# A two-layer graph network: the last batch's preparation, the order of its norm, values and products, and where single-value transfers are issued

## The chip, the cores and the metric

The kernel runs on one core of one Trainium2 chip. The metric is the device time of one execution in microseconds (us). A core has five engines that run their own instruction queues in order and meet by semaphores: PE (matmul), DVE (vector), ACT (scalar activations), POOL (GpSimd) and SP, which here only issues DMA transfers. POOL and ACT issue transfers too.

## What is computed

Eight batches of 2048 tokens with 256 features, and one 2048 by 2048 adjacency matrix for all. Two layers, each with a norm ahead of it and a residual:

```python
# layer 0: attention in 4 heads, a softmax for each chunk of 256 keys
h = maximum(layernorm(x), 0)
q, k, v = h @ Wq.T + bq, h @ Wk.T + bk, h @ Wv.T + bv      # split into heads
s = clip(q @ k.T / sqrt(64), -10, 10); s = where(adj == 0, -10, s)
ctx = sum over chunks of softmax(s within the chunk) @ v
out = ctx @ Wo.T + bo + h
x = x + layernorm(out) * gamma + beta
# layer 1: one graph-attention step
h = maximum(layernorm(x), 0) @ W
e = leaky_relu(h @ a1 [row] + h @ a2 [column], 0.01); e = where(adj == 0, -1e9, e)
x = x + relu(softmax(e) @ h)
```

A row of `adj` without any neighbour gives equal weights, so such a token gets the mean of all `h` instead.

## The kernel before, in words

Tokens come in four blocks of 512 (`NNB` = 4), called zero, low, mid and last; a block is four tiles of 128 tokens. The instruction order on each engine is written by hand: what the program emits first on an engine runs first there. Tiles of one tag share a few buffers, and an instruction that takes a buffer waits for the last user of it.

**Setup.** The first batch is projected to q, k and v; in between, `find` turns rows of `adj` into flags (DVE, with a copy on POOL), `bound` turns them over on PE and has ACT write them as int8 bounds (`keep_bounds`, line 314). Parts that don't stay on the chip are put on a list, and `send_bounds` (line 304) issues them to DRAM from POOL. It is called at the end of each `find` and once more at the end of the setup. The pieces `att.early(0..3)` start the attention meanwhile; `early(2)` holds the first sum on POOL.

**Attention frames.** Attention runs in steps, one for each pair of block and key chunk, 32 a batch. `begin(f)` and `end(f)` form frame f, f = 2 to 34: logits of one step (line 503), clip on DVE (543), exponentials on ACT (552), sums of pairs on POOL (`both`, 558), value products on PE (519), sums on PE (531), reciprocals on ACT (563, 564), scaling on DVE (573), and `gather` (578), a transfer from POOL that accumulates into `ctxT`. All other work is put beside it by half-frame: `at(n, piece)` has the piece run in frame n // 2, in its second part where n is odd. `PER` is 16 half-frames for a block and `STEPS2` is 64.

A block's work between the layers is in the class `Between`: `load` fetches x; `residual` makes the layer's input again by the first norm (ACT, line 379); `bias` and `beta` add two constant rows to it and to x (lines 748, 772); `output` multiplies the context by Wo; `take` (741) adds residual and output; `stats`, `power`, `shift`, `scaled`, `gamma` (768) and `add` (776) are layer 0's last norm; `stats1`, `power1`, `shift1`, `norm1` are layer 1's first. In the frames `bias`, `beta`, `gamma` and `add` run on POOL, after them on DVE. `beside()` gives the half-frames for blocks zero, low and mid, counted from the end of the block's own steps. Block last has its load, residuals, bias and beta in the frames around n = 58 to 69.

**Between the layers.** After the frames comes a list for each engine order, one for batches with a next one (`ahead`) and one for the last batch. `flip1`, `send1` and `fetch1` turn a normed block by way of DRAM; `ends(0)` turns it on PE instead (`turn1`, `keep1`, line 799), `ends(1)` makes the four tiles of h (`values`, line 827) and keeps them (`keep`: ACT 835, DVE 836). Layer 1's scores need e by row and by column: `targets` works on columns (ACT 916, 917); rows go through DRAM as single values (`send`, line 921, 512 values of four bytes) and come back to all partitions (`receive`, line 925, then `received`, line 934), or by PE (`sources`).

**Layer 1.** `weights(i)` (DVE, lines 953 and 959) makes the i-th of 16 tiles of weights: four pairs of instructions in two halves. `products(i)` (PE, line 976) multiplies it: 32 matmul records; i = 4 nb + j4 for query block nb and quarter j4 of the keys. In the last quarter PE goes by token groups, and a group needs both halves of the weights. In the last batch `early(i)` does products 0 to 2 before the loop. `mean` (PE 903, ACT 907) makes the average row, `alone(nb)` (DVE) adds it to tokens without neighbours, `finish` (994 to 999) scales and adds on POOL. In the last batch the loop starts at i = 3.

Of the kernel before, what the change touches and what calls it, by code (L numbers as in the profile page):

```python
# [28 lines left out]
def gnn_two_layers(  # L29
# [656 lines left out]
    class Between:  # L686
# [160 lines left out]
                    self.values(t)  # L847
                    self.keep(t)

        def beside(self):  # L850

            todo = {
                -3: [self.load],
                3: [lambda: self.residual(0)],
                4: [lambda: self.residual(1)],
                5: [lambda: self.bias(0)],
                6: [lambda: self.bias(1)],
                8: [pe(lambda: self.output_tiled(0)), lambda: self.stats([0]), lambda: self.beta(0)],
                9: [
                    pe1(lambda: self.output_tiled(1)), after_clips(lambda: self.take(0)),  # L860
                    after_clips(lambda: self.take(1)), lambda: self.stats([1]),
                ],
                10: [lambda: self.stats([2]), lambda: self.beta(1)],
                11: [lambda: self.stats([3])],
                12: [self.power],
                13: [self.shift],
                14: [lambda: self.scaled(range(TB))],
                15: [lambda: self.gamma(0)],
                16: [lambda: self.gamma(1)],
                18: [lambda: self.add(0)],  # L870
                20: [lambda: self.add(1)],
            }

            def at(n, *pieces):
                todo.setdefault(n, []).extend(pieces)

            if self.nb == NNB - 2:
                return todo
            at(22, lambda: self.stats1([0]))

            at(25, first(lambda: self.stats1([1, 2, 3])))
            at(26, self.power1)
            at(27, self.shift1)
            at(28, lambda: self.norm1(0))
            at(29, lambda: self.norm1(1))
            at(30, lambda: self.flip1(0))
            at(31, lambda: self.flip1(1))
            at(33, self.send1)
            return todo
# [217 lines left out]
    find(20, 21)  # L1107
    bound(18, 19)
    proj.qk(NNB - 1, 1)
    att.early(2)  # L1110
    bound(20, 21)
    find(22, 23)
# [35 lines left out]
    for b in range(B):  # L1148
# [21 lines left out]
            of[HALVES_OF[k % 8]] = fetch_bounds(HALVES_OF[k % 8])  # L1170

        for nb in range(NNB - 1):
            for n, pieces in blocks[nb].beside().items():
                at((nb + 1) * PER + n, *pieces)
        if b == 0:
            for n, pieces in once.items():
# [14 lines left out]
                at(n + 7, lambda nb=nb: ahead.send(nb))  # L1191
        for k in range(8):
            at(8 * k + (40 - 24 if b == 0 and k == 3 else 12), lambda k=k: fetch(k + 3))
        at(STEPS2 - 6, last.load)
        at(STEPS2, lambda: last.residual(0))

        late = 0 if ahead else 2
        at(STEPS2 + 1 + late, lambda: last.residual(1))
        at(STEPS2 + 2, lambda: last.bias(0))
        at(STEPS2 + 3 + late, lambda: last.bias(1))  # L1200
        at(STEPS2 + 4, lambda: last.beta(0))
        at(STEPS2 + 5, lambda: last.beta(1))
        at(STEPS2 + 3, low.fetch1)
        if ahead:
            at(STEPS2 - 4, lambda: ahead.fetch(0))
# [29 lines left out]
        if ahead:  # L1235
            for t in range(TB):
                mid.stats1([t])
                low.values(t)
                low.keep(t)
            low.sum1()  # L1240
            zero.fetch1()
            mid.power1()
            mid.shift1()
            mid.norm1(0)
            mid.norm1(1)
            ahead.values(0)
            ahead.fetch(2)
            last.output(0)
            last.output(1)
            mid.flip1(0, "both")  # L1250
            last.take(0)
            mid.flip1(1)
            last.take(1)
            mid.send1()
            zero.sum1()
            last.stats(range(TB))
            ahead.qk(1, 0)
            last.power()
            last.shift()
            last.scaled(range(TB))  # L1260
            ahead.qk(1, 1)
            for t2 in range(2):
                last.gamma(t2)
                last.add(t2)
            for t in range(TB):
                last.stats1([t])
                zero.values(t)
                zero.keep(t)
            mid.fetch1()
            last.power1()  # L1270
            last.shift1()
            last.norm1(0)
            last.norm1(1)
            ahead.values(1)
            ahead.qk(2, 0)
            last.flip1(0, "both")
            last.flip1(1)
            last.send1()
            ahead.fetch(3)
            mid.sum1()  # L1280
            ahead.qk(2, 1)
            mid.ends(1)
            last.fetch1()
            one.send(1)
            one.send(2)
            ahead.values(2)
            one.receive(1)
            one.targets(0, 3 * TB)
            one.sources(0)
            ahead.qk(3, 0)  # L1290
            weights(0)
            ahead.qk(3, 1)
            last.sum1()
            last.ends(1)
            one.total()
            one.targets(3 * TB, NT)
            weights(1)
            one.send(3)
            ahead.values(3)
        else:  # L1300
            one.targets(0, TB)
            one.sources(0)
            weights(0)
            low.ends(1)
            low.sum1()
            mid.stats1(range(TB))
            mid.power1()
            mid.shift1()
            accs[0] = one.accumulators(0)
            early(0)  # L1310
            mid.norm1(0)
            mid.norm1(1)
            one.targets(TB, 2 * TB)
            last.output(0)
            last.output(1)
            weights(1)
            last.take(0)
            last.take(1)
            mid.ends(0)
            mid.ends(1)  # L1320
            last.stats(range(TB))
            last.power()
            last.shift()
            last.scaled(range(TB))
            one.targets(2 * TB, 3 * TB)
            one.send(1)
            one.receive(1)
            for t2 in range(2):
                last.gamma(t2)
                last.add(t2)  # L1330
            last.stats1(range(TB))
            last.power1()
            last.shift1()
            weights(2)
            fetch(11)
            last.norm1(0)
            last.norm1(1)
            early(1)
            last.ends(0)
            last.ends(1)  # L1340
            early(2)
            one.total()
            one.targets(3 * TB, NT)
            weights(3)
            one.mean()
            one.received(1)
            one.send(2)
            one.send(3)
            one.receive(2)
            weights(4)  # L1350
            fetch(12)
# [4 lines left out]
        for i, (nb, j4) in enumerate(pieces1):  # L1356
            if not ahead and i < 3:
                continue
            if i + 2 < len(pieces1):
                weights(i + 2)  # L1360
            if i % 2 == 0 and (ahead or i < 10):
                fetch(i // 2 + 11)
            if nb not in accs:
                accs[nb] = one.accumulators(nb)
            if j4 == 1 and nb + 1 < NNB:
                one.received(nb + 1)
                if nb + 2 < NNB:
                    one.receive(nb + 2)
            if j4 == 2:
                one.alone(nb)  # L1370
            one.products(accs[nb], ws.pop(i), j4)
            if ahead and i == 0:
                one.mean()
            if j4 == 0 and nb > 0:
                one.finish(nb - 1, accs[nb - 1])
            if j4 == 1 and nb > 0:
                one.store(nb - 1)
            if far and i in (3, 6, 9, 12):
                far.send(i // 3 - 1)
            if far and i in (0, 3, 6, 9):  # L1380
                far.load(i // 3)
            if far and i in (1, 4, 7, 10):
                far.stats(i // 3, range(TB))
                far.power(i // 3)
                far.shift(i // 3)
            if far and i in (2, 5, 8, 11):
                for t2 in range(2):
                    far.norm(i // 3, t2)
                for t2 in range(2):
                    far.flip(i // 3, t2)  # L1390
            if ahead and i == len(pieces1) - 4:
                att = Attention(ahead)
            if ahead and i >= len(pieces1) - 4 and i < len(pieces1) - 1:
                att.early(i - (len(pieces1) - 4))
                if i == len(pieces1) - 2:
                    att.early(3)
# [34 lines left out]
```

## Time and profile before

| what | value |
|---|---|
| median of 3 runs | 3537.56 us (3534.24, 3537.56, 3537.88) |
| the profiled execution, own time | 3534.5 us |
| its span, first to last instruction | 3532.7 us |
| PE busy | 3512.5 us, 99% |
| DVE busy | 2632.9 us, 75% |
| ACT busy | 1945.8 us, 55% |
| POOL busy | 1825.8 us, 52% |
| bytes moved | 330.29 MB, mean 93 GB/s |

The profile gives, for one execution, when each instruction ran on its engine and what released it. A line of a timeline has the start, the time, the engine, the source line, the operation, the tiles it writes and reads, and in brackets how long the engine was idle before and what ended that. "x32" means so many instructions put together. A line of the waits has who waited for whom, the total in us, the number of times and the longest. The clock is the share of full speed that PE was granted; over the span its mean was 0.999.

### The profile page before, as it was taken

How to read it: one execution, taken by the hardware profiler on the slowest of the kernel's cores; microseconds unless marked ns; L12 is line 12 of the kernel's file. 1: busy time of each engine (PE TensorE's matmuls, PEld its weight loads, DVE VectorE, ACT ScalarE, POOL GpSimd, SP SyncE). 2: the span in 40 equal slices, each digit the busy share in tenths (PEclk: the TensorE clock that was granted, in tenths of full speed). 3: DMA queues.
4: the chain of work that ended last, by engine and by line, in shares of the span. 5: the costliest groups of instructions: out<-in, count | busy, mean ns of one | idle time of the engine just before them, and what ended most of it. 6: DMA issues, size and time to landing. Idle time of an engine off the chain costs nothing.

```text
span 3532.7 us, 104631 instructions
## 1 busy us (share of the span) xinstructions
PE 3512.5 (99%) x46104; PEld 2370.3 (67%) x46104; DVE 2632.9 (75%) x3979; ACT 1945.8 (55%) x2961; POOL 1825.8 (52%) x1198
## 2 busy tenths in 40 slices
PE   9999999999999999999999999999999999999989
PEld 5455775667777687566867758656686665855768
DVE  6887677877678676786767868678586785867866
ACT  6777426763267633676236762477624766047740
POOL 5677017870278602785037850378404883058731
PEclk9999999999999999999999999999999999999999
DMA  7545323443144431444324343243432434223421
GB/s 245 126 109 123 93 84 75 97 114 98 62 92 86 115 99 61 92 92 109 97 66 88 86 121 104 61 84 81 120 99 67 86 83 114 60 61 80 102 62 45
DMA packets 178521, 330.29 MB, mean 93 GB/s; under 512 B 36752, under 2 KB 98448, under 8 KB 178064
## 3 DMA queue, kind: packets, MB, share of 16 engines
q1 hardware_dynamic: 136912, 203.51, 18.9%
q0 software_dynamic: 32832, 119.03, 18.4%
q8 instruction: 361, 5.91, 0.7%
q10 hardware_dynamic: 8320, 1.05, 0.2%
q14 instruction: 96, 0.79, 0.1%
HBM read 154.67 MB, written 51.43 MB: 58 GB/s over the span
## 4 chain that ended last, share of the span: by engine, by line
PE 98%; DVE 1%; ACT 1%; DMA 0%; issue 0%; POOL 0%; ACTq 0%; DVEq 0%; POOLq 0%
PE ps_s L503 25%; PE ps_n L519 25%; PE ps_s L976 12%; PE ps_t L531 7%; PE ps_n L976 6%; PE ps_t L976 6%; PE ps_t L727 2%; PE ps_t L447 2%; PE ps_n L447 2%; PE ps_s L447 2%; PE ps_n L827 2%; PE ps_t L827 2%; PE ps_n L461 1%; PE ps_t L461 1%; PE ps_t L705 0%; PE ps_n L705 0%
## 5 line engine op out<-in xcount | busy, mean ns | idle before, releaser
L543 DVE SCALAR_TENSOR_TENSOR e<-ps_s,bound 128x1024 f32<-128x1024 f32 x1024 | 1217.6, 1221 | 399.8 <-PE ps_s L503 395.7
L558 POOL TENSOR_TENSOR both<-e 128x1024 f32<-128x1024 f32 x512 | 1220.2, 2410 | 546.9 <-PE ps_t L531 238.1
L503 PE MATMUL ps_s<-q,k 64*32 64x512 f32 x16384 | 1328.4, 590 | 0.1
L552 ACT ACTIVATE e<-e 128x1024 f32<-128x1024 f32 x1024 | 1049.2, 1049 | 453.9 <-DVE e L543 436.3
L519 PE MATMUL ps_n<-e,v 64*32 64x512 f32 x16384 | 1114.6, 589 | 2.1 <-DVE prod L573 1.4
L503 PEld LDWEIGHTS ps_s<-q,k 64*32 64x32 f32 x16384 | 524.0, 106 | 386.5 <-issue 248.7
L519 PEld LDWEIGHTS ps_n<-e,v 64*32 64x32 f32 x16384 | 556.9, 107 | 332.0 <-issue 200.0
L531 PE MATMUL ps_t<-both,ones 64*32 64x512 f32 x4096 | 553.2, 590 | 0.0
L976 PE MATMUL ps_s<-g,w 128*128 128x257 f32 x2048 | 450.2, 381 | 5.0 <-DVE w L959 5.0
L976 PEld LDWEIGHTS ps_s<-g,w 128*128 128x128 f32 x2048 | 389.4, 190 | 61.8 <-DVE w L959 5.4
L573 DVE TENSOR_TENSOR prod<-ps_n,rz 128x512 f32<-128x512 f32 x448 | 288.9, 687 | 133.4 <-ACT rz L564 70.9
L999 POOL TENSOR_TENSOR x<-x,r 128x256 f32<-128x256 f32 x124 | 90.7, 745 | 469.3 <-ACT r L997 468.5
L959 DVE SCALAR_TENSOR_TENSOR w<-bound,w 128x1024 f32<-128x1024 int8 x256 | 314.7, 1229 | 8.7
L367 POOL TENSOR_TENSOR krn<-krn,mv 128x4 f32<-128x4 f32 x28 | 6.8, 243 | 571.7 <-DVE w L953 571.7
L976 PE MATMUL ps_n<-g,w 128*128 128x257 f32 x1024 | 292.4, 382 | 0.0
L976 PE MATMUL ps_t<-g,w 128*128 128x257 f32 x1024 | 289.8, 380 | 0.0
L563 ACT ACTIVATE rz<-ps_t 128x512 f32<-128x512 f32 x256 | 152.6, 596 | 226.2 <-PE ps_t L531 140.3
L953 DVE TENSOR_SCALAR w<-src,cd 128x512 f32<-128x512 f32 x512 | 268.7, 567 | 9.9 <-ACT src L934 7.0
L531 PEld LDWEIGHTS ps_t<-both,ones 64*32 64x32 f32 x4096 | 156.3, 105 | 100.5 <-SPq L475 43.8
L976 PEld LDWEIGHTS ps_n<-g,w 128*128 128x128 f32 x1024 | 192.8, 190 | 44.3 <-issue 17.6
L578 POOL DMA_DIRECT2D ctxT<-prod x224 | 191.0, 853 | 53.4 <-DVE prod L573 46.9
L976 PEld LDWEIGHTS ps_t<-g,w 128*128 128x128 f32 x1024 | 193.8, 189 | 28.2
(139 smaller groups left out, 2970.1 us busy)
## 6 DMA issues: line engine op xcount, KB each, us to landing
ctxT<-prod POOLq DMA_DIRECT2D x224, 512.0 KB, 4.9
bound<-bound_d SPq DMA_DIRECT2D x125, 512.0 KB, 4.8
turned_d<-squares SPq DMA_DIRECT2D x232, 128.0 KB, 2.9
hT<-turned_d SPq DMA_DIRECT2D x58, 512.0 KB, 4.5
rows<-in_adj_dram SPq DMA_DIRECT2D x32, 512.0 KB, 5.2
x<-in_x_dram SPq DMA_DIRECT2D x32, 512.0 KB, 6.4
out_dram<-x SPq DMA_DIRECT2D x31, 512.0 KB, 2.6
xp<-in_x_dram SPq DMA_DIRECT2D x28, 512.0 KB, 4.3
```

The source lines that it names most:

```text
L447: nc.tensor.matmul(in_key_order(pp) if i == 0 else pp, w[:, di, do * P:(do + 1) * P], h, start=di == 0, stop=di == FC - 1,)
L503: nc.tensor.matmul(self.s[n, o][c * Q:(c + 1) * Q, kt, :], self.k[p][rows, at:at + Q], self.q[p][rows, nb * NB:(nb + 1) * NB], start=True, ...
L519: made.append(nc.tensor.matmul(self.num[n, c][h * Q:(h + 1) * Q, :], self.v[rows, j * KT + kt, at:at + Q], self.e[n, p][rows, i * KT + kt, :],
L531: nc.tensor.matmul(self.total[n][h * Q:(h + 1) * Q, :], ones[rows, :], self.both[n, h // 2][rows, h % 2, :], start=half == 1, stop=half == 0,)
L543: nc.vector.scalar_tensor_tensor(self.e[n, p][:, i * KT:(i + 1) * KT, :], self.s.pop((n, o)), -CLIP * SC, bounds[nb, j // 4][:, j % 4 * KT ...
L552: nc.scalar.activation(e, e, AF.Exp, scale=1.0 / SC)
L558: nc.gpsimd.tensor_tensor(self.both[n, p], e[:, 0], e[:, 1], op=ALU.add)
L573: nc.vector.tensor_tensor(dst[:, c, :], self.num.pop((n, c)), self.rz[n], op=ALU.mult)
L578: nc.gpsimd.dma_start(self.ctxT[nb], self.prod.pop(n), accum_op=ALU.add)
L953: nc.vector.tensor_scalar(w[:, i, :], self.src[nb], self.cd[:, 0, j:j + 1], self.cd[:, 1, j:j + 1], op0=ALU.mult, op1=ALU.max,)
L959: nc.vector.scalar_tensor_tensor(two, bounds1[nb, j // 8][:, j % 8 - 1:j % 8 + 1, :], 0.0, two, op0=ALU.is_gt, op1=ALU.mult)
L976: nc.tensor.matmul(accs[t][:, 0:F + 1], w[:, i, t * P:(t + 1) * P], g[:, j, :], start=j == 0, stop=j == NT - 1,)
```

## The change

- In the setup, one more call of `send_bounds()` stands between the last projection of k and `att.early(2)`.
- In the last batch block mid's two `add` pieces move from half-frames 66 and 68 to 65 and 66.
- In the last batch block last's seven pieces move: load from 58 to 37, residuals from 64 and 67 to 42 and 43, bias from 66 and 69 to 49 and 51, beta from 68 and 69 to 59 and 60. In the other batches the list has the half-frames that they had.
- In batches with a next one, `send(1)` moves ahead, right behind block mid's `send1`; `send(2)` moves behind `weights(1)`.
- In the last batch's list, block mid's values and keeps are put around the `power` and `shift` of block last, `weights(2)` and a fetch of bounds stand ahead of block last's `scaled`, and products 1 and 2 come earlier: 1 ahead of `stats1`, 2 ahead of block last's `ends`. The mean moves behind products 3, in the loop.
- In the last batch `alone(0)` is added behind it. Before, the loop skipped i = 2, where this step stands.

```diff
+            soon = soon and self.nb == NNB - 2
+            at(17 if soon else 18, lambda: self.add(0))
+            at(18 if soon else 20, lambda: self.add(1))
...
     proj.qk(NNB - 1, 1)
+    send_bounds()
     att.early(2)
...
-            for n, pieces in blocks[nb].beside().items():
+            for n, pieces in blocks[nb].beside(soon=ahead is None).items():
...
-        at(STEPS2 - 6, last.load)
-        at(STEPS2, lambda: last.residual(0))
-
-        late = 0 if ahead else 2
-        at(STEPS2 + 1 + late, lambda: last.residual(1))
-        at(STEPS2 + 2, lambda: last.bias(0))
-        at(STEPS2 + 3 + late, lambda: last.bias(1))
-        at(STEPS2 + 4, lambda: last.beta(0))
-        at(STEPS2 + 5, lambda: last.beta(1))
+        early_parts = [58, 64, 65, 66, 67, 68, 69] if ahead else [37, 42, 43, 49, 51, 59, 60]
+        last_parts = [
+            last.load, lambda: last.residual(0), lambda: last.residual(1), lambda: last.bias(0),
+            lambda: last.bias(1), lambda: last.beta(0), lambda: last.beta(1),
+        ]
+        for n, piece in zip(early_parts, last_parts):
+            at(n, piece)
...
             mid.send1()
+            one.send(1)
             zero.sum1()
...
             last.fetch1()
-            one.send(1)
-            one.send(2)
             ahead.values(2)
...
             weights(1)
+            one.send(2)
             one.send(3)
...
             mid.ends(0)
-            mid.ends(1)
             last.stats(range(TB))
-            last.power()
-            last.shift()
+            for t in range(TB):
+                if t == 2:
+                    last.power()
+                    last.shift()
+                mid.values(t)
+                mid.keep(t)
+            one.targets(2 * TB, 3 * TB)
+            weights(2)
+            fetch(11)
             last.scaled(range(TB))
-            one.targets(2 * TB, 3 * TB)
             one.send(1)
             one.receive(1)
             for t2 in range(2):
                 last.gamma(t2)
                 last.add(t2)
+            early(1)
             last.stats1(range(TB))
             last.power1()
             last.shift1()
-            weights(2)
-            fetch(11)
             last.norm1(0)
             last.norm1(1)
-            early(1)
+            early(2)
             last.ends(0)
             last.ends(1)
-            early(2)
             one.total()
             one.targets(3 * TB, NT)
             weights(3)
-            one.mean()
             one.received(1)
...
             one.products(accs[nb], ws.pop(i), j4)
-            if ahead and i == 0:
+            if i == (0 if ahead else 3):
                 one.mean()
+            if not ahead and i == 3:
+                one.alone(0)
```

More of the change, by code (lines that the diff above doesn't have):

```diff
@@ L848, in ends, with beside @@
                     self.keep(t)
-        def beside(self):
+        def beside(self, soon):
             todo = {
@@ L869, in beside @@
                 16: [lambda: self.gamma(1)],
-                18: [lambda: self.add(0)],
-                20: [lambda: self.add(1)],
             }
```

## The prediction

> **What bounds the kernel now.** I read the page's slices and chain first, then the waits of PE, then PE's timeline around its gaps, and there DVE, POOL and ACT.
>
> From the page, the slices and the chain by engine:
>
> ```profile
> PE   9999999999999999999999999999999999999989
> ...
> PE 98%; DVE 1%; ACT 1%; DMA 0%; issue 0%; POOL 0%; ACTq 0%; DVEq 0%; POOLq 0%
> ```
>
> PE is the bound nearly everywhere; only slice 39 (3356 to 3444 us) falls below nine tenths. So an edit counts only where PE now idles, or where it newly makes PE idle. The waits of PE alone say where (total, times, longest):
>
> ```profile
> PE ps_s L976 <- DVE w L959: 5.0, 1, 5.0
> PE ps_n L388 <- ACT hn L379: 4.6, 1, 4.6
> ...
> PE ps_n L519 <- ACT bound_part L314: 0.8, 1, 0.8
> ```
>
> The first two lie between the two layers of the last batch. PE's timeline there:
>
> ```profile
> 3387.86 1.03 PE L827 MATMUL ps_t<-w1s,hT 128*128 128x258 f32 x4
> 3393.85 8.74 PE L976 MATMUL ps_s<-g,w 128*128 128x257 f32 x32 [4.96 <-DVE w L959]
> ...
> 3410.99 7.10 PE L976 MATMUL ps_s<-g,w 128*128 128x257 f32 x32
> 3422.71 1.95 PE L388 MATMUL ps_n<-ident,hn 128*128 128x128 f32 x4 [4.61 <-ACT hn L379]
> ...
> 3437.94 7.12 PE L976 MATMUL ps_s<-g,w 128*128 128x257 f32 x32
> ```
>
> The same 32 products take 8.74 and 7.10 us. The table by stretches, cut where the clock changes, has the reason (columns: PE, PEld, DVE, ACT, POOL busy, granted clock, DMA share, GB/s):
>
> ```profile
> 3393.58:3397.00 3.42, 3.15 (x7) 2.51 (x8) 3.35 (x11) 0.00 (x0) 0.00 (x0) 0.50 0.00 0
> ...
> 3417.47:3420.89 3.42, 0.63 (x3) 0.19 (x2) 3.18 (x11) 0.00 (x0) 0.00 (x0) 1.00 0.00 0
> 3420.89:3427.71 6.82, 4.95 (x13) 3.15 (x14) 4.57 (x8) 4.31 (x12) 0.00 (x0) 0.50 0.00 0
> ```
>
> After each gap PE runs at half clock, 3.4 and 6.8 us long. Why the first gap exists, from DVE's and POOL's timelines:
>
> ```profile
> 3386.11 6.43 DVE L953 TENSOR_SCALAR w<-src,cd 128x512 f32<-128x512 f32 x2 [0.43 <-ACT src L934]
> ...
> 3393.72 1.00 DVE L953 TENSOR_SCALAR w<-src,cd 128x512 f32<-128x512 f32 x2
> ```
>
> ```profile
> 3385.98 0.86 POOL L578 DMA_DIRECT2D ctxT<-prod  x1 [5.60 <-DVE prod L573]
> 3386.58 1.56 POOL L776 TENSOR_TENSOR x<-x,o 128x512 f32<-128x512 f32 x1
> ...
> 3390.26 1.53 POOL L772 TENSOR_TENSOR x<-x,beta_r 128x512 f32<-128x512 f32 x1
> ```
>
> The same pair takes 6.43 us beside four POOL additions and 1.00 us without them; one instruction took 5971 ns against a median of 541, until POOL ended at 3391.79. The third wait is in the setup:
>
> ```profile
> 69.00 3.54 POOL L304 DMA_DIRECT2D bound_d<-bound_part  x4
> 74.03 1.94 ACT L314 ACTIVATE bound_part<-ps_z 128x1024 int8<-128x1024 bf16 x2 [3.94 <-DMA bound_d<-bound_part]
> 76.02 2.45 PE L519 MATMUL ps_n<-e,v 64*32 64x512 f32 x26 [0.77 <-ACT bound_part L314]
> ```
>
> ACT waits there for a transfer that POOL issued late, and PE for ACT.
>
> [...] a window that was 18% busy (0.63 of 3.42) lowered the clock too, and one of 60% (2.03 us of 3373.1 to 3376.5) didn't. [...] the 2 KB send of single values lands here after a median 10.2 us.
>
> **The change part by part**, against the profiled execution (3534.5 us, span 3532.7). Times are of its clock.
>
> *Setup, one early send.* ACT finishes the two parts at 62.27 + 1.93 = 64.2, so POOL issues both by 65.2 (0.88 each). They land after at most 6.8 us (longest of this transfer in the trace), by 70.1 and 71, instead of 73.9. ACT, free at 70.1, evicts 22 and 23 by 72.1 and exponentiates by 74; PE wants that at 75.65. The cost: POOL's first sum and the two copies of z behind it come up to 2 us later, the second ending at 69.8 instead of 69.1, so its eight transposes start at 69.85 instead of 69.24: +0.6. From its first logits of frame 2 (73.31) PE issued 96 records until 81.45; at the pace of full frames (32 records in 1.72 us) they need 5.15, so 3.0 us were lost. Now 73.9 + 5.15 = 79.05, and by DVE's second clip (ends 78.2) 79.15. Gain 2.3; bounds -0.6 (only POOL's delay is felt) and 2.9.
>
> *Seven batches with a next one: sends.* One send follows the middle block's turned squares, another goes behind the weights. PE has no idle there (20.00 busy of 2964 to 2984 and of 2984 to 3004). The last block's fetch landed 7.89 us after issue beside two sends, the middle one's 3.51 without, yet at 2995.05 it was early for PE's 2997.69. The send on SP ahead of the middle fetch is issued at about 2964.6 and done near 2975; that fetch starts at 2973.36 (it waits for PE) and is wanted at 2983.44. Cost and gain 0; the early list for these batches equals the old slots.
>
> *Last batch, frames.* The last block's two norms (ACT, 1.08 each) go to half-frames 42 and 43, its four POOL additions to 49, 51, 59, 60, its load to 37. Two additions in one frame exist in the old kernel (POOL at 3253.88 and 3255.13): the sums behind them start 0.06 late. The frame of 59 has two and a shift, 0.55 late, with 0.25 to spare before PE; frame 21 delays ACT's reciprocal by 0.35, which DVE's multiplication half covers. I take +0.2, bounds 0 and 3.
>
> *Last batch, between the layers.* After 3385.98 POOL has only the gather left.
> - DVE's first instruction did not get in at 3386.11 although the first addition began at 3386.58, so I let the gather hold it to 3386.84 (bounds 0 and 0.85). The first half of the weights then ends at 3389.1 (0.54 + 0.52 + 1.22 on), and DVE's chain is 4.67 ahead of before.
> - PE: products 0 from 3389.2 (6.95) to 3396.15, output 3.46 to 3399.6, transposes to 3400.5. The middle block's values need the bank that `take` frees at 3406.90 - 4.67 = 3402.25: a gap of 1.8. Values 3.5 to 3405.8.
> - Only two values go ahead of `power`; ACT and DVE reach weights 2 at 3407.15, done at 3411.6. PE needs them at 3412.75, behind products 1. The old 4.6 us wait for the last norm is covered: DVE goes on at 3411.55, and gamma to norm takes 8.06 as before, so to 3419.6, while products 2 end at 3419.7. Transposes and values as before for the middle block (1.38 + 3.73): 3424.8.
> - What is late next: products 3, with nothing before them now. Weights 3 start 2.12 after the last value matmuls start (before: 3429.26 to 3431.38), at 3426.05; their halves end 2.25 and 4.44 later, 3428.3 and 3430.5. The first token group needs both: PE idles 3.5, runs 0.87, idles 1.3, and ends products 3 at 3430.55 + 6.08 = 3436.65. The mean, moved behind them, 0.87: products 4 at 3437.5, against 3437.94 + 6.95 = 3444.9. Gain 7.4.
> - That new gap will cost clock: a half-clock window costs up to 1.7, part of it inside the gap. I take 1.2; bounds 0.4 and 3.4 (two windows).
> - The four new `alone` steps stand on DVE between weights 5 and 6, behind the mean, done about 3440.5; weights 6 end at 3445, wanted at 3451. Free. `fetch` 11 stands ahead of send 1 and receive 1 on SP, waits for weights 1 until 3401.6; receive lands near 3415, wanted at 3426. Free.
>
> Sum: 2.3 + 7.4 - 1.2 - 0.2 = 8.3, so 3526.2 on the profiled execution's time. The median of the runs, 3537.56, is 3.1 above it; on that, 3529.
>
> **The rivals.**
> - A, the late wait costs more: two half-clock windows (3.4), and the setup gives nothing: 7.4 - 3.4 = 4.0, 3533.5. [...] against: the setup wait has one plain cause.
> - B, POOL wasn't what held DVE: the 4.67 stay, and only the reordering pays: 2.7 + 2.3 - 1.2 = 3.8, 3534. Against: one instruction of 512 took 5971 ns, and it ended with POOL.
> - C, slower: the single-value send stands ahead of the middle block's fetch in seven batches. It decides if that fetch lands over 10.1 us after issue (2983.44 - 2973.36); each us beyond costs 7. At the longest landing of such a send, 12.6, it costs 17.5, so 3546. For: the last fetch took 7.89 beside two; against: this send is nearly done when the fetch starts, so 10.1 isn't near.
> - That the sends don't do what they are moved for: the last fetch will land in about 3.5 instead of 7.9 us, and nothing waits for it. This is in the forecast.
>
> **How the numbers follow.** Forecast 0.72 (own range 3525 to 3532), A 0.14, B 0.08, C 0.06. What can be told from no change is about 0.2%, 7 us, so faster means below 3530.5. Of the forecast's cases about 0.63 lie there, 0.09 above; with A and B that gives faster 0.63, same 0.31, slower 0.06. The range 3524 to 3536 takes in A and B and leaves out C.
>
> **What would show it.** Right: the first pair of the last batch's weights takes 1 to 2 us; the 4.96 and 4.61 waits are gone; a wait of products 3 for weights of 3 to 5 us stands after the last values, then half clock; the setup's products of frame 2 don't wait for a bound part. Wrong: PE gaps in the seven earlier batches (C), a pair still at 6 us (B), or frames 21 to 30 of the last batch over 7.73 us.

## The result, and the profile after

The changed kernel takes 3527.6 us in the median of 11 runs (3524.82 to 3531.08), the kernel before 3536.22 in 11 runs on the same chip (3534.24 to 3537.88). The ratio is 0.9977, its 95% interval 0.9967 to 0.9986: 0.23% faster. The profiled execution took 3525.83 us with a span of 3524.1, 8.6 less than the span before.

The page's slices and chain after:

```profile
PE   9999999999999999999999999999999999999999
...
PE 98%; DMA 1%; DVE 0%; ACT 0%; POOL 0%; issue 0%; ACTq 0%; DVEq 0%; POOLq 0%
```

The slice that was at 8 tenths is full now. The waits of PE after (total, times, longest):

```profile
PE ps_s L977 <- DVE w L960: 3.5, 1, 3.5
PE ps_n L1035 <- POOL ident masks.py:199: 1.5, 1, 1.5
PE ps_n L519 <- DVE prod L573: 1.4, 1, 1.4
```

The waits of 5.0 and 4.6 are gone and one of 3.5 has come; the other two lines stand at the kernel's start and in the last frames, as before. Lines of the kernel behind 876 have moved down by one (953 is 954, 959 is 960, 976 is 977). PE's timeline between the layers of the last batch, after:

```profile
3386.16 1.03 PE L827 MATMUL ps_t<-w1s,hT 128*128 128x258 f32 x4
3387.03 7.10 PE L977 MATMUL ps_s<-g,w 128*128 128x257 f32 x32
...
3398.80 1.28 PE L827 MATMUL ps_n<-w1s,hT 128*128 128x258 f32 x4 [0.34 <-ACT hT L799]
...
3402.53 14.04 PE L977 MATMUL ps_s<-g,w 128*128 128x257 f32 x64
3416.41 0.84 PE L388 MATMUL ps_n<-ident,hn 128*128 128x128 f32 x4
...
3425.40 10.12 PE L977 MATMUL ps_s<-g,w 128*128 128x257 f32 x32 [3.48 <-DVE w L960]
3435.36 1.02 PE L904 MATMUL ps_n<-w1s,hsum 128*128 128x256 f32 x4
```

Products 0 follow the values at once, at full clock (7.10 us, granted clock 1.00). Products 1 and 2 run as one block of 64. Then products 3 (the line at 3425.40) wait 3.48 us and take 10.12. DVE and POOL at the start of weights 0, after:

```profile
3384.41 1.00 DVE L954 TENSOR_SCALAR w<-src,cd 128x512 f32<-128x512 f32 x2 [0.43 <-ACT src L935]
```

```profile
3384.28 0.86 POOL L578 DMA_DIRECT2D ctxT<-prod  x1 [6.82 <-DVE prod L573]
```

The pair that took 6.43 us takes 1.00, although the gather on POOL runs beside it. In the trace of before PE's clock changes between the layers at 3393.58, 3397.00, 3417.47, 3420.89 and 3427.71, which lie whole multiples of 3.41 us apart; a "window" below is one such 3.41 us. The windows around the new wait (columns as in the table of before):

```profile
3420.62:3424.04 3.42, 1.30 (x6) 0.78 (x5) 1.56 (x7) 1.77 (x5) 0.00 (x0) 1.00 0.07 1
3424.04:3427.45 3.41, 2.05 (x4) 1.17 (x4) 3.38 (x5) 0.00 (x0) 0.00 (x0) 0.50 0.23 77
3427.45:3430.87 3.42, 3.30 (x9) 2.67 (x9) 3.35 (x6) 0.00 (x0) 0.00 (x0) 0.50 1.03 80
```

PE was busy for 1.30 of 3.42 us, and two windows at half clock followed.

Where the time came from, read from both traces at four marks on PE:

| stretch | before | after | gain |
|---|---|---|---|
| start to layer 1 of batch 0 | 403.41 | 401.81 | 1.60 |
| six batches, from there to layer 1 of batch 6 | 2601.22 | 2600.67 | 0.55 |
| from there to the last values of block low (line 827) | 383.23 | 383.68 | -0.45 |
| from those values to products 4, "between the layers" | 57.04 | 50.06 | 6.98 |

The gains sum to 8.68; from products 4 to the last instruction both need 87.83 us. One part of the last stretch is chance, as the same wait had different times behind it. Behind the one of 3.5 us for weights 3 PE was at half clock for 6.83 us in the changed kernel and for 3.41 in send2_behind_send3 (below), and behind the wait of 4.96 products 0 took 8.58 us up to the next instruction in the kernel before and 9.47 in sends_only. With the frames and the order of before, this stretch took 57.04 us here and 58.37 in sends_only (below); with those of the changed kernel 50.06 here, 48.99 in send2_behind_send3 and 50.19 in no_setup_send. So differences of up to some 1.3 us between single traces of it say nothing.

### The profile page after: what moved, and what is told of

Its sections match the earlier page's. It is cut to its first block, busy times and chain, and to the rows that moved or that the text cites. A ratio compares the mean times of both kernels' runs of the same rounds, so it can differ in the third digit from the quotient of the medians.

```text
span 3524.1 us, 104630 instructions
## 1 busy us (share of the span) xinstructions
PE 3510.2 (100%) x46104; PEld 2370.7 (67%) x46104; DVE 2628.7 (75%) x3983; ACT 1944.9 (55%) x2961; POOL 1825.0 (52%) x1198
## 4 chain that ended last, share of the span: by engine, by line
PE 98%; DMA 1%; DVE 0%; ACT 0%; POOL 0%; issue 0%; ACTq 0%; DVEq 0%; POOLq 0%
PE ps_s L503 25%; PE ps_n L519 25%; PE ps_s L977 13%; PE ps_t L531 7%; PE ps_n L977 6%; PE ps_t L977 6%; PE ps_t L727 2%; PE ps_t L447 2%; PE ps_n L447 2%; PE ps_s L447 2%; PE ps_n L827 2%; PE ps_t L827 2%; PE ps_n L461 1%; PE ps_t L461 1%; PE ps_t L705 0%; PE ps_n L705 0%
```

## The experiments

Two theories stood against each other for the last batch. Mine: POOL's late additions hold DVE, DVE holds PE, so moving them pays most, and the new order pays something of its own. The rival: the order pays, and the additions hold nothing. Beside that, the setup's send and the sends in the other batches each had a price to be tested. All ratios are against the kernel before on the same chip.

**frames_only.** The kernel before, with the pieces of the last batch's frames moved and nothing else:

```diff
-                18: [lambda: self.add(0)],
-                20: [lambda: self.add(1)],
+            at(17 if soon else 18, lambda: self.add(0))
+            at(18 if soon else 20, lambda: self.add(1))
...
+        early_parts = [58, 64, 65, 66, 67, 68, 69] if ahead else [37, 42, 43, 49, 51, 59, 60]
```

> The kernel before with one part of the change: in the last batch, block mid's adds and block last's load, norms, bias and beta in their new half-frames; nothing else. Theory (POOL's additions hold DVE): with only the gather left on POOL the first pair of the last batch's weights takes about 1.0 us instead of 6.43, PE's 4.96 us wait for weights is gone, products 0 take 7.1 us instead of 8.74, and DVE's chain up to the last norm is 5.4 us ahead. PE then waits longer for that norm (about 6.4 us instead of 4.6), so that 5.4 us are left of it in the whole run. Rival (DVE was held by something else): the pair stays at 6 us and the run at the time of before. Should the moved pieces slow the frames, PE's frames of the last batch exceed 7.73 us.

Measured: 3529.49 us, ratio 0.9979 (0.9969 to 0.9988). DVE's timeline and then PE's of this kernel:

```profile
3385.18 1.00 DVE L954 TENSOR_SCALAR w<-src,cd 128x512 f32<-128x512 f32 x2 [0.43 <-ACT src L935]
```

```profile
3387.80 7.10 PE L977 MATMUL ps_s<-g,w 128*128 128x257 f32 x32
...
3414.96 1.95 PE L388 MATMUL ps_n<-ident,hn 128*128 128x128 f32 x4 [4.55 <-ACT hn L379]
```

DVE's pair took 1.00 us. The first wait is gone, and the wait for the norm stays as it was (6.4 us were expected). Between the layers it took 50.19 us, 6.85 less than before, of 6.98 in the changed kernel. So the moved pieces alone bring nearly all of the gain there; that it is the additions among them, two_adds_back shows.

**order_only.** The kernel before, with the new order of norm, values and products, the mean behind products 3, and `alone(0)`:

```diff
-            mid.ends(1)
...
+                mid.values(t)
+                mid.keep(t)
+            weights(2)
+            fetch(11)
...
+            early(1)
...
+            early(2)
```

> The kernel before with the other part for the last batch: the new order of norm, values and products between the layers, the mean and the added alone step in the loop; the frames as before, so POOL's four additions stay beside the first weights. Theory: the pair still takes 6.4 us and PE still waits 5.0 us for it; the 4.6 us wait for the last norm goes, and a wait for weights 3 of 3 to 4 us comes in its place, so only 1 to 2 us are gained. Rival (the order is what pays, the frames are not needed): 5 us or more.

Measured: 3536.11 us, ratio 1.0 (0.9991 to 1.0008), and 58.08 us between the layers, 1.04 more than before. DVE's timeline and then PE's of this kernel:

```profile
3385.21 6.42 DVE L953 TENSOR_SCALAR w<-src,cd 128x512 f32<-128x512 f32 x2 [0.43 <-ACT src L934]
```

```profile
3434.09 10.25 PE L976 MATMUL ps_s<-g,w 128*128 128x257 f32 x32 [3.48 <-DVE w L959]
```

The additions still hold DVE, and PE waits 4.96 us for weights 0 as before. Behind this wait products 0 took 9.94 us up to the next instruction, against 8.58 before: 1.36 us that the order has no part in and that I put down to the clock (at full clock, in the changed kernel, they took 6.94). Without them it would be 0.3 less than before. The order took the norm's wait of 4.61 us away and put one of 3.48 for the weights in its place, behind which products 3 took 10.25 us, against 7.12 at full clock before. The order pays nothing that can be seen, by itself or on top of the frames (50.19 without it, 48.99 to 50.19 with it). This refutes the rival, and my share for the order.

**two_adds_back.** The changed kernel with two of the four additions (beta) back in their old place:

```diff
-        early_parts = [58, 64, 65, 66, 67, 68, 69] if ahead else [37, 42, 43, 49, 51, 59, 60]
+        early_parts = [58, 64, 65, 66, 67, 68, 69] if ahead else [37, 42, 43, 49, 51, 68, 69]
```

> The changed kernel with block last's two beta additions put back to half-frames 68 and 69, so that POOL has two additions behind the gather instead of none (before: four). Theory [...]: the first pair of the last batch's weights takes 3.5 to 4 us, between 1.0 (none) and 6.43 (four), its first instruction ends about 0.3 us behind POOL's last addition, and the products behind come about 2.9 us later than in the changed kernel. Rival: the pair stays at 1.0 and the time at that of the changed kernel.

Measured: 3531.02 us, ratio 0.9988 (0.9981 to 0.9994). DVE's timeline and POOL's:

```profile
3385.17 4.00 DVE L954 TENSOR_SCALAR w<-src,cd 128x512 f32<-128x512 f32 x2 [0.43 <-ACT src L935]
```

```profile
3385.64 2.78 POOL L772 TENSOR_TENSOR x<-x,beta_r 128x512 f32<-128x512 f32 x2
```

With none, two and four additions the pair took 1.00, 4.00 and 6.43 us: the dose decides, so POOL is the cause. PE waited 2.54 us for weights 0, and between the layers it took 54.36 us, 4.3 more than in the changed kernel: 2.7 up to the start of products 0, and 1.2 in products 3 (11.11 us up to the next instruction against 9.96). There the first records ran at full clock, PE waited 1.07 us more for the second half of the weights, and two half-clock windows stood from 3430.29 to 3437.11.

**sends_only.** The kernel before, with the setup's send and the moved sends of the batches with a next one:

```diff
+    send_bounds()
...
+            one.send(1)
...
-            one.send(1)
-            one.send(2)
...
+            one.send(2)
```

> The kernel before with the early call of send_bounds in the setup and the moved sends of single values in seven batches. Theory: PE reaches the turn of the output weight about 1.7 us earlier (before: 81.45 us), all later batches keep that lead unchanged, and nothing is lost or won between the layers, although the last block's fetch lands in about 4 us instead of 7.9; run 1.7 us shorter, which the rounds can't tell from none. Rival (a send ahead of the middle block's fetch costs PE): the lead shrinks batch by batch.

Measured: 3534.35 us, ratio 0.9993 (0.9984 to 1.0001), which can't be told from no change. In its trace PE lost 2.1 us once, in batch 5, to the last block's fetch, which landed 12.33 us after issue:

```profile
2564.37 1.11 PE L827 MATMUL ps_n<-w1s,hT 128*128 128x258 f32 x4 [2.08 <-DMA hT<-turned_d]
```

`send(2)` stands behind `weights(1)` in the program, but SP doesn't wait for weights: it issued the send 0.94 us behind that fetch, where it had been before. What the change took away there is the other send, 0.42 us behind the fetch.

**send2_behind_send3.** The changed kernel, with `send(2)` held back by what `send(3)` waits for:

```diff
-            one.send(2)
             one.send(3)
+            one.send(2)
```

> Changed kernel, but in the batches with a next one send 2 is issued behind send 3, so some 14 us behind the last block's fetch instead of 0.9 us. If the send close behind the fetch is what makes it land late now and then (10.45 us in one of seven batches of the changed kernel, 10.8 and 12.3 in others with the same order), the fetch lands within 4.2 us in all seven batches and no batch is longer than 433.4 us; PE has no wait for the turned block. Worth 0.3 to 1 us a run. If the late landing has another origin (the rival), one or two batches of the seven still show a landing over 10 us.

Measured: 3526.78 us, ratio 0.9974 (0.9964 to 0.9984). The fetch landed within 4.0 us in six batches and at 5.12 in one. Transfers around that one in batch 5, in a version with the changed kernel's sends (split_weights, below) and then in this one (the last column is us from issue to landing):

```profile
hT<-turned_d SPq DMA_DIRECT2D x1, 512.0 KB, 12.4
src_raw<-source_d SPq DMA_DIRECT2D x1, 256.0 KB, 12.1
source_d<-sd SPq DMA_DIRECT2D x1, 2.0 KB, 11.8
```

```profile
hT<-turned_d SPq DMA_DIRECT2D x1, 512.0 KB, 5.1
src_raw<-source_d SPq DMA_DIRECT2D x1, 256.0 KB, 5.3
```

The fetch, the receive and the send end together in the first, within a us; without the send both others are done after 5. In each of the six traces with the changed kernel's sends, one batch of seven showed this (always batch 5, 9.5 to 12.4 us; the next longest landing is 7.8); in the two traces with `send(2)` held back, none of fourteen did. In the three traces with both sends near, as before, the fetch took over 9 us in 8 of 21 batches, of which one was batch 5. So a near send makes the fetch late now and then; why in those batches stays open. The ratio is 0.0003 below the changed kernel's, which can't be told from nothing.

**no_setup_send.** The changed kernel without the setup's additional call:

```diff
-    send_bounds()
     att.early(2)
```

> Changed kernel without the additional early send of bounds in the setup. The forecast's term says 2.3 us slower than the changed kernel (3529.9), with ACT's 3.9 us wait for the bound parts back and the turn by the output weight starting near 81.4. The rival, from the profiles so far (80.4 to 81.45 without the early send, 79.99 to 80.28 with it): 0.3 to 1.2 us slower, so 3528 to 3529, because the wait it removes was mostly covered for PE.

Measured: 3527.67 us, ratio 0.998 (0.9973 to 0.9988), as fast as the changed kernel. In four traces without the call PE needed 14.21 to 15.49 us from the transposes at 66 us to the turn of the output weight (mean 14.72; the kernel before has 15.49), in seven with it 13.36 to 13.83 (mean 13.65). The call is worth about 1.1 us in the traces, too little for the medians.

**halves_only.** The changed kernel; products 3 of the last batch are taken by halves of the weights, not by token groups:

```diff
-            if 4 * j4 + 4 == NT:
+            if 4 * j4 + 4 == NT and not halves:
                 pairs = [(i, t) for t in range(TB) for i in range(4)]
```

> Changed kernel, but products 3 of the last batch are taken by halves of the weights instead of by token groups; nothing else. If the gain of the split version (6 us) comes from the weights being ready earlier, this edit keeps the 3.5 us wait and the half clock, and products 4 start 0 to 1 us earlier than in the changed kernel (49.19 us behind the first products): the median stays at 3526.5 to 3528. If it comes from PE's order in products 3 (the rival), the distance falls to about 44 us and the median to near 3522.

Measured: 3524.11 us, ratio 0.9967 (0.9955 to 0.9979). PE's timeline, and then the windows of its clock:

```profile
3426.38 8.61 PE L977 MATMUL ps_s<-g,w 128*128 128x257 f32 x32 [3.49 <-DVE w L960]
```

```profile
3422.38:3425.80 3.42, 0.51 (x3) 0.11 (x1) 2.19 (x6) 1.45 (x5) 0.00 (x0) 1.00 0.11 10
3425.80:3429.21 3.41, 2.83 (x7) 2.30 (x8) 3.38 (x6) 0.00 (x0) 0.00 (x0) 0.51 0.25 67
3429.21:3432.62 3.41, 3.41 (x17) 3.00 (x16) 3.34 (x5) 0.00 (x0) 0.00 (x0) 0.99 1.05 94
```

The wait is the same, but one half-clock window follows it instead of two, and from the first products to products 4 it took 47.69 us, not 49.19. PE was busy for 2.83 of the 3.41 us at half clock, in the changed kernel for 2.05. The 1.5 us are more than I had expected; they are clock (and about 0.33 us of idle within products 3), not the wait. But the clock's part isn't shown to come from the halves. In send2_behind_send3, which takes products 3 by token groups like the changed kernel, one window followed too:

```profile
3425.12 9.06 PE L977 MATMUL ps_s<-g,w 128*128 128x257 f32 x32 [3.49 <-DVE w L960]
```

```profile
3421.62:3425.03 3.41, 0.02 (x1) 0.00 (x0) 2.50 (x6) 1.39 (x4) 0.00 (x0) 1.00 0.17 38
3425.03:3428.44 3.41, 3.19 (x7) 2.15 (x8) 3.34 (x6) 0.00 (x0) 0.00 (x0) 0.50 0.11 40
3428.44:3431.86 3.42, 3.42 (x18) 2.97 (x17) 3.39 (x5) 0.00 (x0) 0.00 (x0) 1.00 0.11 12
```

There the gap filled one window, products 3 began with the next, and from the first products to products 4 it took 48.12 us. Against that trace the halves save 0.4 us. The median lies 3.5 us below the changed kernel's, but the intervals of the two ratios overlap.

**split_weights.** The changed kernel, with weights 2 and products 2 cut in two around the last norm and the last values, and products 3 by halves as above:

```diff
-            weights(2)
-            fetch(11)
+            weights(2, 0)
...
             early(1)
+            early(2, 0)
...
             last.shift1()
+            weights(2, 1)
+            fetch(11)
             last.norm1(0)
             last.norm1(1)
-            early(2)
             last.ends(0)
             last.ends(1)
+            early(2, 1)
```

> Changed kernel, but weights 2 are made in two halves around the last block's norm, and PE takes the halves of products 2 before and after the last block's values; products 3 are taken by halves of the weights instead of by token groups. If the late wait of products 3 for their weights (3.5 us in the changed kernel) and the half clock behind it are only a matter of what PE has left to do while DVE makes weights 3, the wait goes or falls below 1 us, products 3 run at full clock, and products 4 start 4 to 6 us earlier than in the changed kernel (3436.2), so the median is near 3523. If instead every order moves a wait of the same size somewhere else (the rival: DVE's and ACT's chain from the norm to the last weights has a fixed length that PE's remaining work cannot cover), PE idles 3 us or more ahead of the last block's transposes, the clock halves there, and the median stays within 1.5 us of the changed kernel.

Measured: 3521.16 us (3520.25 to 3522.34), ratio 0.9961 (0.9949 to 0.9974). PE's timeline:

```profile
3404.16 10.57 PE L978 MATMUL ps_s<-g,w 128*128 128x257 f32 x48
3414.89 0.33 PE L388 MATMUL ps_n<-ident,hn 128*128 128x128 f32 x1 [0.17 <-ACT hn L379]
...
3417.48 1.28 PE L827 MATMUL ps_n<-w1s,hT 128*128 128x258 f32 x4 [0.34 <-ACT hT L799]
...
3421.21 10.83 PE L978 MATMUL ps_s<-g,w 128*128 128x257 f32 x48
3431.88 1.03 PE L904 MATMUL ps_n<-w1s,hsum 128*128 128x256 f32 x4
```

Products 2 and 3 after the last values are 48 records without a gap, at full clock (10.83 us, granted clock 1.00). The 16 records kept back (3.5 us) fill the time in which ACT and DVE make weights 3. DVE makes the second half of weights 2 while ACT normalizes, so its own chain isn't longer. Between the layers it took 44.96 us, 5.1 less than in the changed kernel and 3.6 less than in halves_only (48.57). The intervals of the two ratios overlap a little, but on this chip all five executions are faster than all nine of send2_behind_send3 and all fifteen of no_setup_send. The split with products 3 by token groups wasn't run. There the first group would be done at 3425.7 and need the second half of weights 3, which DVE ended at 3426.9, so by my estimate PE would idle some 1.2 us.

**split_and_send2.** Both edits, the split and `send(2)` behind `send(3)`.

> Both edits at once: weights 2 and products 2 and 3 in halves, and send 2 behind send 3. If they are independent, the gain over the changed kernel is the sum of the two alone, 4.5 to 7 us, near 3522. If the last batch's gain is given back, it stays at 3526 to 3528.

Measured: 3520.86 us (3520.05 to 3523.22), ratio 0.9961 (0.9949 to 0.9974). In its trace (span 3518.2) no batch is longer than 433.41 us, against 435.74 once in the split alone, and between the layers it took 44.95. The gains add in the traces; in the medians the second edit isn't seen. These two are the fastest versions.

## Why the prediction came out as it did

The predicted time, 3529, is 1.4 us above the median measured; the sum of 8.3 stands against 8.68 in the traces. Nearly all of the 1.4 comes from the base: the median of 3 runs that the forecast was set on, 3537.56, is 1.3 above that of 11. The terms of the sum were less right than the sum. Of the signs named beforehand all that speak for it came, and two that speak against it came too, in small: frames over 7.73 us, and a wait of 0.20 us in batch 5.

- *Setup, 2.3: too large.* The traces show 1.1 in the mean. The step that failed is "They land after at most 6.8 us". That bound was the longest of one execution. In the changed kernel the two sends landed after 8.7 us, and the pair ahead of them after up to 8.8; without the call that pair took up to 8.6 (no_setup_send). The timeline of ACT after, with part 21 in the first line and 22 and 23 in the second:

```profile
71.25 1.02 ACT L314 ACTIVATE bound_part<-ps_z 128x1024 int8<-128x1024 bf16 x1 [2.34 <-DMA bound_d<-bound_part]
72.57 1.94 ACT L314 ACTIVATE bound_part<-ps_z 128x1024 int8<-128x1024 bf16 x2 [0.30 <-PE ps_t L461]
```

  ACT evicted 22 and 23 from 72.57 on, not from 70.1. In all eleven traces, with the call and without, PE began to turn the output weight 7.42 to 7.45 us after ACT began with part 22. So it is the landing that sets the gain. Also, the profiled execution I worked from was the slowest here of the four without the call, by 0.7 us: part of what stands there as "3.0 us were lost" was that execution.
- *Sends, 0: right in sum, its reason wrong.* "PE has no idle there" I had read from one batch. Of the seven batches before, batch 1 lost 1.0 us: the last fetch landed 11.30 us after issue, so by my estimate (11.30 less 1.0) PE can bear about 10.3 there. The change made that rarer (batch 5 alone), not impossible. Rival C, the middle fetch behind the early send, didn't come: that fetch landed after 4.1 to 5.2 us in the changed kernel, far from the 10.1 at which it would have cost.
- *Frames, -0.2: small, as said, but -0.45.* Three frames in a row have two additions each, and the delay of one carries over to the next; the third took 8.07 us, not 7.72, by the start of PE's sums (line 531). By PE's logits (line 503) all of the 0.45 is lost in this frame and the two beside it. A later frame's sums came 0.28 us late too, but its logits took 7.72 as before, so it cost nothing.
- *The gather holds DVE to 3386.84, 0.73: wrong.* DVE's pair took 1.00 us beside the gather. Only the additions hold it (4.00 us with two of them, 6.43 with four).
- *"a gap of 1.8" for the bank that `take` frees: wrong.* Values began at 3398.80, before `take` at 3399.10, and waited only for the turned block.
- *Norm and products 2 covered: right.* Products 2 ended as the norm was ready, with no wait.
- *What is late next, products 3: right.* A wait of 3.5 us was forecast and 3.48 measured. Counted from the last values of block low, products 3 began 1.2 us earlier than forecast, since the two costs above (the gather and `take`) weren't there.
- *Clock: 1.3 idle and 1.2 for the clock.* It was about 0.33 idle and two windows: products 3 took 9.96 us instead of 6.95, so 2.7 us are the clock's. That lies between the 1.2 taken and the upper bound (3.4), and is the two windows of rival A. In send2_behind_send3 one window followed a wait of the same length: PE was busy for 0.02 us of the window before it, not 1.30, and products 3 took 8.89 us, with 1.6 us of clock.
- *The order's own share, 2.7 in rival B: wrong.* It pays nothing alone, as a wait of 3.48 us, with products 3 at 10.25 us behind it, takes the place of the 4.61 and its 6.82 us at half clock. The total held because the frames' share, 4.7 by that count, was too small: they bring 6.85, with the whole wait of 4.96 and the half clock of products 0 behind it (8.74 us against 7.10: 1.6).

So the mechanism named first (POOL's additions hold DVE and DVE holds PE) is shown by removal, by return and by dose. That the sum came so near is in part luck: terms of opposite sign were off.

## What to carry to other kernels

A wait that a new order takes away must be followed to the next one: here 4.6 us for the norm became 3.5 for the weights, and the cure was to keep back just so much of PE's work as the other engines need. Before crediting an order, ask which engine's chain is late; moving POOL's work out of a stretch of two engines gave 6.85 us, the reordering alone none. And a place in the program is no delay for a queue that waits for nothing there: the moved send was issued 0.94 us behind the fetch, where it had been. Nor is the longest time of one trace a bound: 6.8 us for a landing became 8.8 in another, and took a part of the setup's gain.

## What the runs showed of the hardware

- In seven waits between the layers the stretch at half clock that followed lasted 3.41 to 3.42 us (the first of the kernel before, halves_only, send2_behind_send3) or 6.82 to 6.83 (the second of the kernel before, frames_only, two_adds_back, the changed kernel), so one window or two. In the window just ahead of it PE was busy for 0.00 and 0.63 us (before), 0.02 (send2_behind_send3), 0.51 (halves_only), 0.75 (frames_only), 0.99 (two_adds_back) and 1.30 (changed kernel). A first window at half clock with 1.47 us busy (frames_only), 1.54 (before), 2.05 (changed kernel) or 2.34 (two_adds_back) was followed by a second; behind one with 2.83 (halves_only), 3.15 (before) or 3.19 (send2_behind_send3) the full clock was back. So in these seven the fuller first windows were the ones that stayed single, and the same order of products 3 had two (changed kernel) and one (send2_behind_send3), with its wait in another place of the windows.
- A 2 KB send of single values, issued by SP 0.94 us behind a 512 KB fetch, came with a late end of that fetch (9.5 to 12.4 us after its issue instead of some 4) in 6 of 42 batches here; with the send some 14 us behind this came in none of 14.
- DVE's first weights instruction ended 0.29 us behind the end of POOL's additions (3391.79 to 3392.08 before), although by the records it had begun 0.47 us ahead of the first. It took 5.97 us against a median of 0.54, so it was held for a whole run of additions, not for one. By what means the additions hold it, no run here shows.
